# Where the outer sums of a fast matrix product, and the differences of GCN weights, stand in VectorE's queue

## The chip, the cores and the metric

The kernel runs on one core of one Trainium2 chip. The metric is device time of one launch in microseconds (us). TensorE (PE in the profile, PEld for its weight loads) multiplies, VectorE (DVE) and ScalarE (ACT) do elementwise work, GpSimd (POOL) and SyncE (SP) mostly issue DMAs.

## The reference, cut to what matters

Four layers on x of 1250 nodes by 1024 features, each added to its input after a layer norm: a graph attention layer, a feed-forward layer, a graph convolution (GCN) and a mixture of 8 experts. All numbers are float32. The change lies in the second layer and prepares the third:

```python
# feed-forward: two small block-diagonal maps ("rails"), gelu, and one big projection
y = jnp.einsum('btri,hrij->bthrj', xr, rail_maker)
z = jnp.einsum('bthrj,hrkj->bthrk', y, rail_up_proj)
h = jax.nn.gelu(z.reshape(b, t, -1), approximate=False)     # 1250 x 16384
out = h @ w_cproj.T                                         # 1250 x 1024
...
# GCN: one dense 1024 x 1024 map, then a weighted sum over edges
h = jnp.einsum('nd,od->no', x, W) + b
```

## The kernel before, in words

The projection `h @ w_cproj.T` is the longest part: it fills the span from about 420 us to about 2215 us. Its 16384 inner features are cut into `NB` = 16 blocks of 1024. A block is a product of a 1024x1024 weight piece X and a 1024x1250 piece Y of the hidden rows. Both are cut into 2x2 blocks, and each of those into 2x2 again, and the products are taken by Strassen's method (Winograd's form): seven products of sums in place of eight. The outer level's products are numbered p (order `OUTER` = 1, 2, 6, 7, 4, 5, 3), the inner level's i. So a block has 7 x 7 = 49 *steps*, each one call of `product`, with 128x128 by 128x313 matmuls into a PSUM tile `po`. In the last block (number 15, from step `end` = 15 x 49 on) the inner level is done directly, in four steps of two products each for every p.

Three kinds of work go with the steps on VectorE, all of them `tensor_tensor` in float32:

- **Sums ahead of products** (`add_up`, L715): the factors' sums and differences, such as `s1 = 21 + 22`. `projection_plan` gives each a step at which it is to be traced, about 11 us of matmuls ahead of the product that needs it. A 128x512 sum is one of X, a 128x626 one is of Y.
- **Outer sums** (`outer_sums`, L776): the results of the products of blocks 0 to 14 are added up by DMA into the DRAM tensor `acc_d` (`accumulate`: ScalarE copies `po` to SBUF, L731, and a GpSimd DMA adds it, L735). Towards the end each p's seven tiles of `acc_d` are loaded back by `load_sums(p)` (L769, on SyncE's queue) and combined by seven 128x626 additions. The list `bring` says from which step on the additions of each p are traced, and how many a step. In the last block the products are added to these by `combine` (L790 and L795).
- **Differences of GCN weights** (`sum_quarters`, L753 to L756): in blocks 2 to 5 four quarters of the GCN weight are loaded at step 24 of the block (`load_quarters`, L749), and at step 31 four differences of them are taken and written to the DRAM tensor `ws_d` (L758), from where the third layer reads them after the projection.

The tiles share storage: `X`, `low`, `arena`, `BZ` and `first_w` are large SBUF tensors cut into slots (`XS` and `YS`), and the lists `xw` and `yh` hold the free ones. Weights come by SyncE's queue too (`load_weights`, L515). So the order in which slots are given out, and what a slot's next user has to wait for, follow from the order in which the steps are traced.

The order on each engine is not the order of the text. A scheduler that knows estimated times puts the traced instructions into each engine's queue, and it may put one that it thinks ready ahead of others traced before it. An engine then takes its queue strictly in that order: an instruction whose input has not come holds up all that stand behind it. The text can bind the scheduler: inside `with tc.issue_after(ins):` every instruction traced for `ins`'s engine is queued behind `ins`.

Of the kernel before, what the change touches and what calls it, by code (L numbers as in the profile page):

```python
# [15 lines left out]
ALU = mybir.AluOpType  # L16
# [33 lines left out]
OUTER, INNER = (1, 2, 6, 7, 4, 5, 3), (1, 2, 5, 6, 7, 4, 3)  # L50
# [52 lines left out]
def gnn_ffn_kernel(ctx, tc, x, src, dst, gat_w, a_l, a_r, maker, up, cproj,  # L103
# [395 lines left out]
    tt = nc.vector.tensor_tensor  # L499
# [9 lines left out]
    def load_weights(b, o, i):  # L509

        (oo, ok), (io, ik) = corner[o], corner[i]
        r0, c0 = b * D + (2 * ok + ik) * 256, (2 * oo + io) * 256
        k = b, "X", o, i
        buf[k] = xw.pop(0)
        nc.sync.dma_start(XS[buf[k]], cproj[r0:r0 + 256, c0:c0 + 256].rearrange("(q p) o -> p q o", p=P))  # L515
# [29 lines left out]
    with tc.tile_pool(name="aps", bufs=6, space=PSUM) as aps, tc.tile_pool(name="tps0", bufs=2, space=PSUM) as tps:  # L545

        def attend(h, b, between=iter(())):
            po = [aps.tile([R, F + 1], F32, name="po") for _ in range(HT)]
            ws = {}
            for s in range(T):  # L550
                with tc.issue_after(z_copied.ins) if h == b == 0 else nullcontext():
                    ws[s] = first_weights.pop(0) if first_weights else weight(h, b, s)

                for i, v in [(i, s) for i in range(HT)] if s < T - 2 else [(i, v) for i in range(HT) for v in (s - 1, s)] if s == T - 1 else ():
                    nc.tensor.matmul(po[i], ws[v][:, i * R:(i + 1) * R], Z[h // 2][:, v, h % 2, :],
                                                 start=(v == 0), stop=(v == T - 1))
                with tc.issue_after(weighed[-1]):
                    next(between, None)
            rs = small.tile([R, HT], F32, name="rs")

            for group in (range(2), range(2, HT)):
                for i in group:
                    nc.scalar.activation(rs[:, i:i + 1], po[i][:, F:F + 1], AF.Copy, bias=1.0e-30)
                nc.vector.reciprocal(rs[:, group[0]:group[-1] + 1], rs[:, group[0]:group[-1] + 1])
            for i in range(HT):
                xs = X[:, b * HT + i, h * F:(h + 1) * F]
                end = nc.vector.scalar_tensor_tensor(xs, po[i][:, :F], rs[:, i:i + 1], xs, op0=ALU.mult, op1=ALU.add)
            return end
# [19 lines left out]
        with tc.tile_pool(name="al", bufs=2) as lnp:  # L588
# [12 lines left out]
            end = attend(3, 0)  # L601
# [45 lines left out]
    with nullcontext(ctx) as tail:  # L647
# [16 lines left out]
        tt = nc.vector.tensor_tensor  # L664
# [5 lines left out]
        def used(k):  # L670
            left[k] -= 1
            if left[k] == 0:
                (xw if k[1] == "X" else yh).append(buf.pop(k))

        def place_y(top):

            return yh.pop(yh.index(max(yh)) if top else 0)

        def view(k):
            return (XS if k[1] == "X" else YS)[buf[k]]  # L680

        def hidden(b, n, k):

            pz = zps.tile([P, 4, 512], F32, name="pz2")
            for q in range(4):
                hidden_rows(pz[:, q, :NQ], b, n, k, q)
            for i in range(2):
                key = b, "Y", f"{k + 1}{n // 2 + 1}", f"{i + 1}{n % 2 + 1}"
                buf[key] = place_y(b == NB - 1 and n > 1)
                nc.scalar.activation(view(key), pz[:, 2 * i:2 * i + 2, :NQ], AF.Gelu)  # L690
# [19 lines left out]
        def add_up(k, sign, src):  # L710
            a = [view(v) for v in src]
            for v in src:
                used(v)
            buf[k] = xw.pop(0) if k[1] == "X" else place_y(k[0] == NB - 1)
            tt(view(k), *a, op=ALU.add if sign == "+" else ALU.subtract)  # L715

        def product(pairs):
            po = ops.tile([P, 2, 512], F32, name="po2")
# [23 lines left out]
        def quarter(i):  # L742
            return YS[i].rearrange("p q n -> p (q n)")[:, :512]
# [7 lines left out]
        def sum_quarters(k):  # L751
            y11, y21, y12, y22 = (quarter(i) for i in pair)
            tt(y11, y12, y11, op=ALU.subtract)  # L753
            tt(y12, y22, y12, op=ALU.subtract)
            tt(y22, y22, y11, op=ALU.subtract)
            tt(y21, y22, y21, op=ALU.subtract)  # L756
            for j, v in enumerate((y11, y22, y12, y21)):
                nc.sync.dma_start(ws_d[j, k], v)  # L758
            yh.extend(pair)


        def free_acc(v):
            (yh if v < 32 else early).append(v)
# [7 lines left out]
        def outer_sums(p):  # L771

            a = {i: acc.pop((p, i)) for i in INNER}
            for d, x, op, y in ((2, 1, ALU.add, 2), (6, 1, ALU.add, 6), (7, 6, ALU.add, 7), (4, 7, ALU.subtract, 4),
                                (6, 6, ALU.add, 5), (3, 6, ALU.add, 3), (5, 7, ALU.add, 5)):
                tt(YS[a[d]], YS[a[x]], YS[a[y]], op=op)  # L776
                yield
            for i, j in (("11", 2), ("12", 3), ("21", 4), ("22", 5)):
                acc[p, i] = a[j]
            for j in (1, 6, 7):  # L780
                free_acc(a[j])
# [79 lines left out]
        end = (NB - 1) * 49  # L861
        last, j = None, 0
        loads_at = dict(zip((end + v for v in (-13, -6, 1, 7, 12, 15, 20)), OUTER))
        bring = [(end + v, k, outer_sums(w)) for v, k, w in zip((-9, 0, 3, 10, 14, 18, 22), (2, 2, 2, 4, 4, 3, 3), OUTER)]
        added, sent, pair = [], [], []
        norm = {}
        for n, (b, p, i, pairs) in enumerate(steps):
            m = n - 49 * b
            if n >= end - 70:

                xw[:] = [v for v in xw if v < 33]
            for w in (b, b + 1):
                while coming.get(w) and len(xw) > (0 if w == b else 16 if m < 12 else 8 if m < 20 else 4):
                    load_weights(w, *coming[w].pop(0))
            if b == 0:
                for v in first.get(m, ()):
                    hidden(0, *v)
            while j < len(sums) and sums[j][0] <= n:
                add_up(*sums[j][1:])
                j += 1  # L880
            if b == 0 and m in late:
                late_tile(late[m])
                if late[m] == T - 1:
                    xw += range(33, 41)
            if 2 <= b < 6:
                if m == 24:
                    load_quarters(b - 2)
                if m == 31:
                    sum_quarters(b - 2)
            if b + 1 < NB:  # L890
                if m == 20:
                    for k in range(2):
                        load_rails(b + 1, k)
                if m in (28, 30):
                    rails(m // 2 - 14, zps.tile([P, 4, 512], F32, name="pz2")[:, 0, :P])
                if m in later:
                    hidden_visit(b + 1, later[m])
            assert n != end - 13 or all(v < 33 for k, v in buf.items() if k[1] == "X")
            if n in loads_at:
                load_sums(loads_at[n])  # L900
            if n == end:
                blocks.close()
                tl = rest.enter_context(tc.tile_pool(name="tl", bufs=2))
                psp = rest.enter_context(tc.tile_pool(name="tps3", bufs=2, space=PSUM))
                yh += parts
            if b == NB - 1:
                while m >= 14 and [v for v in xw if not 8 <= v < 16] and len(W3) < len(quarters):
                    load_quarter()
                if m == 23:
                    nc.gpsimd.dma_start(bias, gcn_b.partition_broadcast(R))  # L910
                while m >= 16 and len(fetched) < 4 and fetch(len(fetched)):
                    pass
                if m == 22:
                    add_out(0)
                    level(0)
                if m == 24:
                    turn_tile(0)
                if m == 27:
                    add_out(1)
                    level(1)  # L920
                    tt(bias[:, 512:], bias[:, 512:], bias[:, :512], op=ALU.subtract)
            po = product(pairs)
            if last:
                (combine if last[0] == NB - 1 else accumulate)(*last[last[0] == NB - 1:])
            for n0, k, sums_of in bring:
                if n0 <= n:
                    with tc.issue_after(added[-1]) if n > end else nullcontext():
                        for _ in range(k):
                            next(sums_of, None)
            last = b, p, i, po  # L930
# [220 lines left out]
    with back_end:  # L1151
# [160 lines left out]
        with tc.tile_pool(name="ops7", bufs=2, space=PSUM) as ops:  # L1312
# [9 lines left out]
            with tc.If(if_late > 0):  # L1322
                with tc.tile_pool(name="lw", bufs=1) as lwp, tc.tile_pool(name="lps", bufs=1, space=PSUM) as lps:
                    for e in range(NE):
                        a, b, c = w1[e], w2[e], w3[e]
# [66 lines left out]
```

## Time and profile before

| What | Value |
|---|---|
| Time, median of 3 runs | 2744.56 us (2742.64, 2744.56 and 2751.24) |
| The profiled execution's own time | 2747.47 us |
| Its span in the trace | 2745.7 us |
| PE busy | 2709.5 us, 99% of the span |
| DVE busy | 1579.3 us, 58% |
| ACT, POOL busy | 906.2 us and 775.8 us |
| L776 | 49 additions of about 0.80 us, from 2001.0 us to 2201.9 us |
| L753 to L756 | 16 differences of about 0.69 us, from 701.3 us to 1048.0 us |

The span is the time from the first to the last instruction of the trace; the execution's own time is a little longer. Times in a trace are counted from the span's start. In a row of the timeline the first number is the start and the second the duration; what stands in brackets is how long the engine had sat idle before it, and on what it had waited.

### The profile page before, as it was taken

Reading aid. Unit: us, or ns where it says so; the run is one execution under the profiler, and the core shown is the slowest. Engines: PE = TensorE matmul, PEld = TensorE weight load, DVE = VectorE, ACT = ScalarE, POOL = GpSimd, SP = SyncE. Lnnn points to the kernel's source line nnn. Section 1 sums busy time; section 2 is a strip of 40 time slices with the busy share of each in tenths; the row PEclk is TensorE's granted clock in tenths of the full one; section 3 lists DMA queues with packets and bytes.
Section 4 is the critical chain, followed back from the end, with each engine's and each line's share of the span. In section 5 each row is a group of like instructions: output and inputs, shape, how many; then the busy total and the mean of one; then the engine's idle time right before and its main releaser. Section 6 shows DMA issues by size and latency. Waiting matters only on the chain. (4 is left out here: it accounts for less than half of the span.)

```text
span 2745.7 us, 32205 instructions
## 1 busy us (share of the span) xinstructions
PE 2709.5 (99%) x11189; PEld 1893.0 (69%) x11189; DVE 1579.3 (58%) x2708; ACT 906.2 (33%) x1611; POOL 775.8 (28%) x1016
## 2 busy tenths in 40 slices
PE   8999999999999999999999999999999999999998
PEld 6678886676676666766667667666676754675676
DVE  9668988564646556645655556455546765431322
ACT  2333345434434344344343443443432011210000
POOL 2000001243443434434344334343442110112131
PEclk9999999999999999999999999999999999999999
DMA  6336216499999999999999999999998540452784
GB/s 186 92 84 180 71 39 228 164 201 172 210 205 177 227 182 199 199 166 189 190 159 204 179 173 197 166 192 182 143 227 228 169 92 0 87 119 63 270 298 157
DMA packets 269147, 457.74 MB, mean 167 GB/s; under 512 B 53672, under 2 KB 143952, under 8 KB 268593
## 3 DMA queue, kind: packets, MB, share of 16 engines
q0 software_dynamic: 126896, 278.80, 58.7%
q1 hardware_dynamic: 142072, 176.67, 21.4%
q8 instruction: 97, 1.59, 0.2%
q14 instruction: 82, 0.67, 0.1%
HBM read 180.57 MB, written 277.02 MB: 167 GB/s over the span
## 5 line engine op out<-in xcount | busy, mean ns | idle before, releaser
L735 POOL DMA_DIRECT2D acc_d<-low x686 | 589.7, 860 | 914.4 <-ACT low L731 894.1
L731 ACT COPY low<-po 128x626 f32<-128x626 f32 x735 | 501.0, 682 | 952.8 <-PE po L722 891.8
L722 PE MATMUL po<-X,arena 128*128 128x313 f32 x2208 | 619.4, 427 | 0.0
L722 PEld LDWEIGHTS po<-X,arena 128*128 128x128 f32 x2208 | 415.2, 189 | 175.6 <-ACT low L731 16.0
L722 PE MATMUL po<-low,arena 128*128 128x313 f32 x1520 | 429.7, 428 | 0.0
L722 PEld LDWEIGHTS po<-low,arena 128*128 128x128 f32 x1520 | 285.5, 189 | 121.4 <-ACT low L731 11.6
L722 PE MATMUL po<-X,first_w 128*128 128x313 f32 x776 | 222.1, 428 | 1.8 <-DVE X L715 1.8
L722 PE MATMUL po<-X,BZ 128*128 128x313 f32 x720 | 208.5, 433 | 3.6 <-DVE BZ L715 3.6
L722 PEld LDWEIGHTS po<-X,first_w 128*128 128x128 f32 x776 | 145.7, 190 | 64.7 <-ACT low L731 7.6
L722 PE MATMUL po<-low,first_w 128*128 128x313 f32 x624 | 179.5, 429 | 1.0 <-DVE low L715 1.0
L722 PEld LDWEIGHTS po<-X,BZ 128*128 128x128 f32 x720 | 136.9, 192 | 62.6 <-issue 6.1
L722 PEld LDWEIGHTS po<-low,first_w 128*128 128x128 f32 x624 | 117.9, 190 | 50.8 <-ACT low L731 4.4
L227 PE MATMUL pz<-W,xT 128*125 128x256 f32 (+1 forms) x480 | 142.0, 455 | 0.3 <-ACT xT L160 0.3
L715 DVE TENSOR_TENSOR X<-X 128x626 f32<-128x626 f32 x125 | 101.2, 813 | 67.1 <-PE po L722 58.9
L722 PE MATMUL po<-low,BZ 128*128 128x313 f32 x480 | 137.6, 427 | 0.0
L715 DVE TENSOR_TENSOR arena<-arena 128x512 f32<-128x512 f32 x126 | 86.3, 687 | 65.6 <-PE po L722 63.1
L227 PEld LDWEIGHTS pz<-W,xT 128*125 128x125 f32 x480 | 90.0, 190 | 43.8 <-issue 33.8
L715 DVE TENSOR_TENSOR X<-X,low 128x626 f32<-128x626 f32 x105 | 85.3, 816 | 56.2 <-PE po L722 46.0
L722 PEld LDWEIGHTS po<-low,BZ 128*128 128x128 f32 x480 | 90.1, 189 | 38.2 <-ACT low L731 3.7
L715 DVE TENSOR_TENSOR X<-low,X 128x626 f32<-128x626 f32 x101 | 81.7, 813 | 53.3 <-PE po L722 49.0
L707 ACT ACTIVATE X<-pz 128x626 f32<-128x626 f32 (+8 forms) x220 | 101.6, 524 | 17.9 <-PE pz L537 17.9
L715 DVE TENSOR_TENSOR low<-X 128x626 f32<-128x626 f32 x100 | 80.9, 811 | 38.3 <-PE po L722 31.1
(304 smaller groups left out, 3383.6 us busy)
## 6 DMA issues: line engine op xcount, KB each, us to landing
acc_d<-low POOLq DMA_DIRECT2D x735, 313.0 KB, 6.2
arena<-in_cproj SPq DMA_DIRECT2D x148, 256.0 KB
w<-in_w SPq DMA_DIRECT2D x16, 1024.0 KB
BZ<-in_cproj SPq DMA_DIRECT2D x56, 256.0 KB
first_w<-in_cproj SPq DMA_DIRECT2D x52, 256.0 KB
w3t<-in_w SPq DMA_DIRECT2D x8, 1024.0 KB
low<-acc_d SPq DMA_DIRECT2D x19, 313.0 KB
X<-acc_d SPq DMA_DIRECT2D x19, 313.0 KB
```

The costliest lines, as they stand in the source:

```text
L227: made_z = nc.tensor.matmul(pz, xT[:, k, t * R:(t + 1) * R], W[hs[0] // 2][:, k, i:i + len(hs)], start=(k == 0), stop=(k == KD - 1))
L707: nc.scalar.activation(view(key)[:, :, n0 - n * NQ:n1 - n * NQ], pz[:, 2 * i:2 * i + 2, a + n0 - c0:a + n1 - c0], AF.Gelu)
L715: tt(view(k), *a, op=ALU.add if sign == "+" else ALU.subtract)
L722: nc.tensor.matmul(po[:, o, :NQ], view(x)[:, q, o * P:(o + 1) * P], view(y)[:, q, :], start=(i == q == 0), stop=(i + 1 == len(pairs) and q ...
L731: nc.scalar.copy(part, po[:, :, :NQ])
L735: sent[:] = [nc.gpsimd.dma_start(out=acc_d[p - 1, i - 1], in_=part, accum_op=ALU.add).ins]
```

## The change

It does three things. The list `summed` now holds the last instruction that `add_up` traced. The four differences of `sum_quarters` are traced inside `issue_after(summed[-1])`, so they are queued on VectorE behind the sums traced ahead of them. The outer sums of p = 1 are traced from step `end` - 4 on, where it was `end` - 9, and they, too, are queued behind the last sum traced; before step `end` and at it they had been bound to nothing. The outer sums of the other p, which come later, are bound to `combine`'s last addition, as they were. The arithmetic and the number of instructions stay as they were.

```diff
@@ add_up
-            tt(view(k), *a, op=ALU.add if sign == "+" else ALU.subtract)
+            summed[:] = [tt(view(k), *a, op=ALU.add if sign == "+" else ALU.subtract).ins]
@@ the loop's lists
-        bring = [(end + v, k, outer_sums(w)) for v, k, w in zip((-9, 0, 3, 10, 14, 18, 22), (2, 2, 2, 4, 4, 3, 3), OUTER)]
-        added, sent, pair = [], [], []
+        bring = [(end + v, k, outer_sums(w)) for v, k, w in zip((-4, 0, 3, 10, 14, 18, 22), (2, 2, 2, 4, 4, 3, 3), OUTER)]
+        added, sent, pair, summed = [], [], [], []
@@ in the loop over steps
                 if m == 31:
-                    sum_quarters(b - 2)
+                    with tc.issue_after(summed[-1]):
+                        sum_quarters(b - 2)
@@ after the product of a step
                 if n0 <= n:
-                    with tc.issue_after(added[-1]) if n > end else nullcontext():
+                    with tc.issue_after((added or summed)[-1]):
                         for _ in range(k):
                             next(sums_of, None)
```

## The prediction

> **What bounds the kernel now.** I read the page's first part: PE is busy in 99% of the span, and the chain that ended last runs through PE up to 2658 us, with a tail of DMA and GpSimd work behind it. So only what PE waits for is worth anything. The waits of PE by line are therefore next:
>
> ```profile
> PE 2709.5 (99%) x11189; PEld 1893.0 (69%) x11189; DVE 1579.3 (58%) x2708; ACT 906.2 (33%) x1611; POOL 775.8 (28%) x1016
> ```
> ```profile
> PE po L722 <- DVE BZ L715: 3.6, 1, 3.6
> PE pt L159 <- DVE arena L151: 2.5, 1, 2.5
> ...
> PE po L722 <- DVE X L715: 1.8, 1, 1.8
> ...
> PE po L722 <- DVE low L715: 1.0, 1, 1.0
> ```
>
> In the whole projection (L722) PE waited three times, each time for a sum of L715. What held up VectorE? Its timeline before the longest of the three:
>
> ```profile
> 2037.79 0.81 DVE L776 TENSOR_TENSOR low<-arena,low 128x626 f32<-128x626 f32 x1 [15.75 <-DMA low<-acc_d]
> ...
> 2068.76 0.81 DVE L776 TENSOR_TENSOR arena<-arena 128x626 f32<-128x626 f32 x1 [15.06 <-DMA arena<-acc_d]
> 2069.48 0.69 DVE L715 TENSOR_TENSOR first_w<-BZ,arena 128x512 f32<-128x512 f32 x1
> 2071.13 0.81 DVE L776 TENSOR_TENSOR arena<-arena 128x626 f32<-128x626 f32 x1 [0.96 <-DMA arena<-acc_d]
> ...
> 2077.17 0.68 DVE L715 TENSOR_TENSOR BZ<-arena 128x512 f32<-128x512 f32 x1
> ```
>
> VectorE stood still for 15.75 and 15.06 us at outer sums of p = 1 whose tiles had not come back from DRAM, with sums for products queued behind them. The sum ending at 2077.85 is what PE waited for, as PE's timeline shows:
>
> ```profile
> 2072.13 2.27 PE L722 MATMUL po<-X,first_w 128*128 128x313 f32 x8
> 2078.00 4.04 PE L722 MATMUL po<-X,BZ 128*128 128x313 f32 x8 [3.60 <-DVE BZ L715]
> 2081.87 2.27 PE L722 MATMUL po<-X,arena 128*128 128x313 f32 x8
> ```
>
> The two short waits have the other cause. Here are VectorE's and then SyncE's timeline in block 3:
>
> ```profile
> 814.10 0.69 DVE L753 TENSOR_TENSOR X<-X 128x512 f32<-128x512 f32 x1 [9.31 <-DMA X<-in_gcn_w]
> ...
> 823.46 0.69 DVE L754 TENSOR_TENSOR X<-X 128x512 f32<-128x512 f32 x1 [5.42 <-DMA X<-in_gcn_w]
> ...
> 826.12 0.81 DVE L715 TENSOR_TENSOR low<-low,X 128x626 f32<-128x626 f32 x1
> ```
> ```profile
> 799.08 5.78 SPq L749 DMA_DIRECT2D X<-in_gcn_w  x3
> 814.82 0.33 SPq L758 DMA_DIRECT2D ws_d<-X  x1
> 815.24 0.38 SPq L749 DMA_DIRECT2D X<-in_gcn_w  x1
> ```
>
> The fourth quarter's load stands on SyncE's queue behind the write of the first difference, which waits for L753. So VectorE waits twice in a row, and PE then waits for the sum at 826.12.
>
> **The change, part by part.** No instruction is added or removed; the built order of both programs tells what moves.
>
> *Differences of weights.* On VectorE L753 moves behind five sums, which had run at 814.71 to 817.36. They now fit into the 9.31 us before L753 (five at 0.6 to 0.7 us: 3.5 us). On SyncE the four loads become neighbours; the first write (L758) moves behind the two weight loads that followed (816.75 and 817.18), so it goes out some 3 us later. Nobody waits for it: `ws_d` is read after the projection. The two weight loads lose a blocker.
>
> When does the fourth load land? Not shown in this place, so I bound it. From below: the time from issue to the end of VectorE's wait for it, 8.2 us here (815.24 to 823.46) and 7.4 us in block 4. From above: 16.5 us, block 4's longest (first load issued 910.48, L753 started 926.96). The third issue ends at 804.86, so the landing lies between 812.3 and 821.4, plus whatever its slot makes it wait; I take the middle, 817. The need: PE could have begun the waiting product at 825.87 (a group of two L532 matmuls before it takes 0.21 us, as at 821.22). In the new order L754 is followed by a sum, L755 and the sum needed, which ends 2.75 us after L754's start; PE starts 0.14 us after that (826.93 to 827.07). So L754 may start as late as 823.0, and even the upper bound leaves 1.6 us. The wait goes. Block 4 has the same order of instructions; its deadline is 937.28 - 2.89 = 934.4 against 916.3 + 16.5 = 932.8. Start to start PE lost 827.07 - 825.87 = 1.20 us and 939.26 - 937.28 = 1.98 us, and each first group after it ran 0.08 us slow (2.19 for 2.11 us). Gain: **3.34 us**. In blocks 2 and 5 PE did not wait: 0.
>
> *Outer sums of p = 1.* All seven move behind the sum that stood at 2079.10 in VectorE's queue. Each sum that was held up at 2037.79 and 2068.76 now goes ahead, the one ending at 2077.85 among them. It needs only weights and sums; between 2053.6 and 2068.76 VectorE was idle, and the ten sums from 2069.48 up to it take 0.6 to 0.7 us each, 6.6 us, so it is done by about 2060, or when its slot comes free. PE's wait goes. Start to start PE lost 2078.00 - 2074.24 = 3.76 us. The next eight matmuls took 3.87 us where 2.11 us is the rule, since the granted clock was low (0.79 on average in 2074 to 2082): 1.76 us more. Gain: **5.52 us**.
>
> What is late next? Behind and among the outer sums stand seven more 128x512 sums of the last blocks (0.61 us apart). If the last tile lands at 2071.13 as before, the seven outer sums (0.73 us each), one outer sum of p = 2 and these seven end at 2071.1 + 5.8 + 4.3 = 2081.2; before, the last of them ended at 2085.7. The last block's first product was at 2092.8, and with 8.9 us gained it is at 2083.9. So 2.7 us remain if the loads come no earlier. They should: SyncE reached them (2058.94) only after a 9.02 us issue of a weight load at 2049.80, which follows PE's progress. The other 42 outer sums stay bound to `combine`. At the step `end` itself p = 2's outer sums were free and are now bound to the last sum; their tiles landed just in time (waits of 0.62 and 0.74 us), and I price that at 0, with 1 us each way.
>
> *The clock.* After the 3.60 us gap the clock was halved; it was halved too after the 2.53 us gap at 2195 (0.76 in 2195 to 2202), and not after gaps of 1.03 and 1.81 us. That third gap I leave: VectorE is busy 4.95 of 5 us before it, with the last tiles' additions and a layer norm, which the change does not touch. [...]
>
> *Sum.* 3.34 + 5.52 = 8.86 us of the profiled execution's 2747.47 us. Everything after 2215 us hangs on PE's progress and follows. That execution is 2.9 us above the median of the runs. The runs lie 8.6 us apart, and waits for DMAs that end just in time are the likely reason. I take the gain off the median: 2744.56 - 8.86 = **2735.7 us**; off the profiled execution it is 2738.6 us.
>
> **Rivals.**
>
> *The outer sums' wait only moves.* The tiles land later than 2071.1 by more than the margin of 2.7 us, since the DMA engines are busy throughout there (share 1.08 in 2074 to 2082), and last-block products wait in place of the earlier one. For: loads before had waits of 15 us. Against: the sums at stake come 4.5 us earlier than before with unchanged landings. At 8 us late PE loses the 5.3 us beyond the margin, and the time is 2735.7 + 5.3 = 2741.0 us.
>
> *The fourth quarter becomes the wait, in four blocks: slower.* All sums behind L754 now wait in one place. If the load lands d us after 823.0 and its like in blocks 2, 4 and 5, PE loses d each time: 4d - 8.86. That decides against the kernel from d = 2.2 us, and by over 0.3% from 4.3 us, a landing 22.4 us after the third issue. At d = 6 us: 2759.7 us. For it: block 4's 16.5 us come within 1.6 us of the deadline, and a slot that frees late adds to it. Against: no load of this kind in the trace took 17 us.
>
> *The change does nothing that lasts.* The profiled waits are of that execution alone and typical ones have fewer: 2744.6 us. Against it: the queue order that makes them is fixed at build time.
>
> **How the numbers follow.** About 0.3% (8.2 us) is what a measurement of this kernel can tell from no change: bounds 2736.3 and 2752.8 us. The forecast gets 0.72; its own range is 2732 (the low clock at 2198 goes as well, 1.8 us, and loads that free up VectorE another 2) to 2738.6 us, and I put 0.54 beyond the bound and 0.18 within it, since executions with longer waits than the profiled one (2751.24 us) gain more. The moved wait gets 0.14, all within. The fourth quarter gets 0.10, slower; nothing that lasts 0.04, half of it within and half slower. So faster 0.54, same 0.34, slower 0.12. The range is 2731 to 2743 us: it takes in the forecast's and the moved wait's times with the unknown 1 us on either end, and leaves out the slow case.
>
> **What would show it.** In the profile after: no wait of PE at L722 for L715; in the blocks 2 to 5 one wait at L753, and one of at most 3 us at L754; four loads L749 as neighbours on SyncE; all outer sums of p = 1 in one stretch at about 2060 to 2076 us with PE busy throughout; the granted clock 1.00 from 423 to 2190 us. I am wrong if PE waits near 2085 to 2100 us, or at L754's place in several blocks, or if PE's gaps go and the time stays.

## The result, and the profile after

| | Before | After |
|---|---|---|
| Time, median | 2744.63 us (22 runs, 2739.6 to 2755.9) | 2754.25 us (22 runs, 2738.88 to 2778.6) |
| Ratio after to before | | 1.0044, 95% interval 1.0028 to 1.006 |
| Profiled execution | 2747.47 us, span 2745.7 us | 2747.03 us, span 2745.3 us |
| PE busy | 2709.5 us | 2707.5 us |
| POOL busy | 775.8 us | 790.0 us |

The change made the kernel slower by 0.44%, where a gain was forecast. Two things in the table point at the cause before any row is read: the times after are spread over 40 us where those before were spread over 16, and GpSimd, whose multiplications the prediction never looked at, is busy for 14.2 us more with the same instructions.

The waits of PE by line, in the profile after (total, times, longest):

```profile
PE po L722 <- ACT low L731: 9.1, 1, 9.1
...
PE pt L159 <- DVE arena L151: 1.1, 1, 1.1
```

The three waits for sums of L715 are gone, as predicted. In their place stands one wait of 9.05 us, for a copy of ScalarE. The chain behind it is followed back engine by engine. PE's timeline in block 5, then ScalarE's:

```profile
1052.59 2.27 PE L722 MATMUL po<-low,arena 128*128 128x313 f32 x8
1063.92 4.28 PE L722 MATMUL po<-low,BZ 128*128 128x313 f32 x8 [9.05 <-ACT low L731]
1068.03 2.27 PE L722 MATMUL po<-X,arena 128*128 128x313 f32 x8
```
```profile
1050.73 0.68 ACT L731 COPY low<-po 128x626 f32<-128x626 f32 x1 [1.43 <-PE po L722]
1063.18 0.68 ACT L731 COPY low<-po 128x626 f32<-128x626 f32 x1 [11.78 <-DMA acc_d<-low]
```

ScalarE had to empty `po` for PE, but it had no free slot to copy into: the slots are given back by the DMAs that add them to `acc_d`. Those are issued by GpSimd. Its timeline:

```profile
1040.70 0.86 POOL L735 DMA_DIRECT2D acc_d<-low  x1 [1.25 <-ACT low L731]
1042.07 14.75 POOL L524 TENSOR_TENSOR BZ<-BZ 128x128 f32<-128x128 f32 x1 [0.51 <-PE pz L532]
1056.79 0.83 POOL L526 TENSOR_TENSOR BZ<-BZ 128x128 f32<-128x128 f32 x1
1057.57 1.76 POOL L735 DMA_DIRECT2D acc_d<-low  x2
```

L524 is a small multiplication of GpSimd in `load_rails`: it spreads a piece of the next block's rail weights over a mask (L526 does the same for the second map). It took 14.75 us. In the profile of before none of the 64 executions of L524 and L526 took over 1.05 us. Behind it in the queue stood the accumulating DMAs, which PE needs every 2.1 us. What did VectorE do meanwhile?

```profile
1036.98 0.69 DVE L754 TENSOR_TENSOR X<-low,X 128x512 f32<-128x512 f32 x1 [3.72 <-DMA low<-in_gcn_w]
1037.59 0.80 DVE L715 TENSOR_TENSOR low<-X 128x626 f32<-128x626 f32 x1
...
1042.39 0.69 DVE L715 TENSOR_TENSOR arena<-arena,first_w 128x512 f32<-128x512 f32 x1
...
1055.87 0.69 DVE L715 TENSOR_TENSOR first_w<-arena,BZ 128x512 f32<-128x512 f32 x1
1056.59 0.77 DVE L715 TENSOR_TENSOR BZ<-arena,first_w 128x512 f32<-128x512 f32 x1
```

It ran sums and differences with two inputs in SBUF, one at the heels of the other, for some 19 us. A 128x512 sum starts 0.60 us after the last one when nothing holds it; the one at 1056.59 reads what the one before wrote and starts after 0.72 us. GpSimd's multiplication ends there, at 1056.82. In the profile of before, the same multiplication and VectorE's neighbours of it are, on GpSimd and on VectorE:

```profile
1045.28 0.40 POOL L524 TENSOR_TENSOR BZ<-BZ 128x128 f32<-128x128 f32 x1 [0.51 <-PE pz L532]
```
```profile
1039.93 0.68 DVE L715 TENSOR_TENSOR BZ<-arena 128x512 f32<-128x512 f32 x1
1045.77 0.83 DVE L754 TENSOR_TENSOR X<-low,X 128x512 f32<-128x512 f32 x1 [5.16 <-DMA low<-in_gcn_w]
```

Before, L524 ran at 1045.28, inside VectorE's 5.16 us of waiting for the fourth quarter. It did so in block 3 (821.7 us) and block 4 (933.1 us) as well. After, in block 5, L754 comes about 9 us earlier, VectorE is through with its waiting when L524 becomes ready, and L524 meets the run of sums. That alone does not hold it: `load_rails` runs twice for each block, and in the profile of before the first L524 of block 2 (711.5 us) and the second one of all four blocks ran beside sums and took 0.62 to 1.05 us. What else it takes, the bench below shows.

The price is read from the starts in PE's timeline: 1063.92 - 1052.59 = 11.33 us where 2.11 us is the rule (9.22 us lost), and 1068.03 - 1063.92 = 4.11 us for the next group at about half the clock (0.53 granted in that stretch; 2.00 us lost). One held multiplication costs **11.2 us**. The windows, with the columns start and end, length, busy time (instructions) of PE, PEld, DVE, ACT and POOL, granted clock, DMA share and GB/s, show the two losses side by side:

```profile
1054.00:1064.00 10.00, 0.95 (x5) 0.38 (x3) 5.06 (x8) 0.68 (x1) 8.70 (x9) 0.68 0.54 98
1064.00:1074.00 10.00, 10.00 (x34) 6.31 (x35) 1.39 (x2) 4.32 (x8) 3.40 (x4) 0.81 1.12 204
```

**Theory A** for the experiments: GpSimd's multiplication is held off by VectorE's unbroken run, and the wait that the change shortens and moves had been its cover. **Theory B**: the outer sums cost the time. **Theory C**, on the bench: beside VectorE, GpSimd loses one instruction's length at most.

### The profile page after: what moved, and what is told of

Same layout as the page of the kernel before. It is cut to its first block, busy times and chain, and to the rows that moved or that the text cites. A ratio compares the mean times of both kernels' runs of the same rounds, so it can differ in the third digit from the quotient of the medians.

```text
span 2745.3 us, 32206 instructions
## 1 busy us (share of the span) xinstructions
PE 2707.5 (99%) x11189; PEld 1891.5 (69%) x11189; DVE 1581.5 (58%) x2708; ACT 906.3 (33%) x1611; POOL 790.0 (29%) x1016
## 5 line engine op out<-in xcount | busy, mean ns | idle before, releaser
L722 PE MATMUL po<-X,arena 128*128 128x313 f32 x2200 | 616.8, 427 | 0.0
L722 PEld LDWEIGHTS po<-X,arena 128*128 128x128 f32 x2200 | 413.8, 189 | 174.8 <-ACT low L731 16.0
L722 PE MATMUL po<-low,arena 128*128 128x313 f32 x1528 | 431.6, 428 | 0.0
L722 PEld LDWEIGHTS po<-low,arena 128*128 128x128 f32 x1528 | 287.0, 189 | 122.0 <-ACT low L731 11.6
L722 PE MATMUL po<-X,first_w 128*128 128x313 f32 x784 | 223.3, 428 | 0.0
L722 PE MATMUL po<-X,BZ 128*128 128x313 f32 x720 | 206.5, 430 | 0.0
L722 PEld LDWEIGHTS po<-X,first_w 128*128 128x128 f32 x784 | 147.1, 189 | 63.1 <-ACT low L731 7.6
L722 PEld LDWEIGHTS po<-X,BZ 128*128 128x128 f32 x720 | 136.0, 191 | 58.2 <-ACT low L731 5.8
L722 PE MATMUL po<-low,first_w 128*128 128x313 f32 x616 | 175.6, 427 | 0.0
L722 PEld LDWEIGHTS po<-low,first_w 128*128 128x128 f32 x616 | 116.0, 189 | 48.9 <-ACT low L731 4.4
L722 PE MATMUL po<-low,BZ 128*128 128x313 f32 x480 | 139.6, 432 | 9.1 <-ACT low L731 9.1
L715 DVE TENSOR_TENSOR X<-X 128x626 f32<-128x626 f32 x125 | 101.3, 814 | 74.2 <-PE po L722 66.0
L715 DVE TENSOR_TENSOR arena<-arena 128x512 f32<-128x512 f32 x126 | 86.8, 690 | 69.2 <-PE po L722 66.7
L722 PEld LDWEIGHTS po<-low,BZ 128*128 128x128 f32 x480 | 91.1, 192 | 48.3 <-ACT low L731 13.2
L715 DVE TENSOR_TENSOR X<-X,low 128x626 f32<-128x626 f32 x106 | 85.7, 811 | 56.7 <-PE po L722 46.0
L715 DVE TENSOR_TENSOR X<-low,X 128x626 f32<-128x626 f32 x100 | 81.2, 817 | 53.4 <-PE po L722 49.0
L715 DVE TENSOR_TENSOR low<-X 128x626 f32<-128x626 f32 x99 | 80.2, 813 | 38.3 <-PE po L722 31.1
```

Source lines behind the costliest of these rows:

```text
L715: summed[:] = [tt(view(k), *a, op=ALU.add if sign == "+" else ALU.subtract).ins]
L722: nc.tensor.matmul(po[:, o, :NQ], view(x)[:, q, o * P:(o + 1) * P], view(y)[:, q, :], start=(i == q == 0), stop=(i + 1 == len(pairs) and q ...
```

## The experiments

### One half of the change each

The kernel with only the outer sums moved and tied (`outer_only`), against the changed kernel:

```diff
-                    with tc.issue_after(summed[-1]):
-                        sum_quarters(b - 2)
+                    sum_quarters(b - 2)
```

> Only the outer sums of p = 1 are moved and tied; the differences of the GCN weights stay where they were in the kernel before. Theory A (a multiplication of the rails on GpSimd, L524, cannot start while VectorE runs sums without a break, and the accumulating DMAs behind it on GpSimd then come late; it was 14.75 us in the changed kernel's block 5, where the differences' wait no longer breaks VectorE's run): the differences' waits and their short PE gaps of 1 to 2 us are back, no L524 above about 1.1 us, no PE gap near 2075 us, so the 5.5 us of that gap are gained: about 2739 us. Theory B (the moved outer sums themselves cost the time, by late tiles or by DMA traffic near the end): as slow as the changed kernel, about 2754 us.

Measured: 2739.87 us (12 runs), ratio 0.9992 to before, interval 0.9982 to 1.0003. Its profile has one wait of PE in the projection, one of the short ones for the differences:

```profile
PE po L722 <- DVE X L715: 0.9, 1, 0.9
```

The kernel with only the differences tied (`quarters_only`):

```diff
-...zip((-4, 0, 3, 10, 14, 18, 22), (2, 2, 2, 4, 4, 3, 3), OUTER)]
+...zip((-9, 0, 3, 10, 14, 18, 22), (2, 2, 2, 4, 4, 3, 3), OUTER)]
...
-                    with tc.issue_after((added or summed)[-1]):
+                    with tc.issue_after(added[-1]) if n > end else nullcontext():
```

> Only the differences of the GCN weights are tied behind the sums; the outer sums stay as before. Theory A: this part carries the whole loss; L524 takes many times its 0.4 to 1 us in some of the blocks 2 to 5, in some executions and not in others, PE waits there for ScalarE's copies, and PE's gap near 2075 us stays: about 2754 + 5 = 2759 us, with runs some 20 us apart. Theory B: 2744.6 - 3.3 = 2741 us, runs close together.

Measured: 2754.35 us (11 runs, 2741.81 to 2778.33), ratio 1.0036, interval 1.0018 to 1.0054: all of the changed kernel's loss and all of its spread. Its profiled execution was its slowest, 2778.33 us, with three held multiplications (15.78, 16.19 and 15.48 us in the blocks 2, 4 and 5) and these waits of PE:

```profile
PE po L722 <- ACT low L731: 30.1, 3, 10.4
PE po L722 <- DVE BZ L715: 3.0, 1, 3.0
```

The second row is the wait behind the outer sums, which this kernel leaves as they were. So theory B falls: the loss comes from the differences' tie alone, and the outer sums' half is harmless at least.

### The changed kernel once more

No edit; a second profile.

> The changed kernel as it is, for a second profile. Theory A: for each multiplication of the rails that takes over 10 us, TensorE has a gap of 9 to 10.5 us in the same block, and the span is the 2735 us that the kernel has without any, plus about 12 to 14 us for each (the gap and the half clock after it). Theory B (the outer sums cost the time): the span does not go with the number of held multiplications.

Measured: 2758.82 us, span 2757.1 us, two held multiplications. GpSimd's timeline in blocks 4 and 5:

```profile
930.57 14.62 POOL L524 TENSOR_TENSOR BZ<-BZ 128x128 f32<-128x128 f32 x1
...
1052.38 15.49 POOL L524 TENSOR_TENSOR BZ<-BZ 128x128 f32<-128x128 f32 x1 [0.51 <-PE pz L532]
```

PE's gaps behind them are 8.85 and 9.72 us. The span is 11.8 us above that of the first profile, which has one. At 11.2 us each, the runs from 2738.88 to 2778.6 us would be runs with none to three or four, out of the four blocks that have differences, and the median one with one or two; only the profiled ones show their number.

### The masks multiplied on VectorE

The changed kernel, and then the kernel before, with L524 and L526 moved:

```diff
-        nc.gpsimd.tensor_tensor(mb.rearrange("p (a b) -> p a b", a=8), ...
+        nc.vector.tensor_tensor(mb.rearrange("p (a b) -> p a b", a=8), ...
...
-        nc.gpsimd.tensor_tensor(ub.rearrange("p (a b) -> p a b", a=2), ...
+        nc.vector.tensor_tensor(ub.rearrange("p (a b) -> p a b", a=2), ...
```

> The changed kernel, with the two multiplications of load_rails (L524 and L526) on VectorE in place of GpSimd, 64 instructions in all. Theory A: GpSimd now only issues DMAs in the projection and is not held up; no PE wait for a copy of L731; what the prediction added up is there: 2735 to 2739 us, runs within some 5 us. Theory B, or any theory in which DMA traffic or the order of the loads delays the accumulating DMAs: still about 2754 us with a wide spread. Against A would also be a GpSimd DMA issue (L735) that takes several us.

Measured: 2735.5 us (7 runs, 2732.58 to 2739.41), ratio 0.9971, interval 0.9958 to 0.9984. No product of the projection (L722) stands among PE's waits. On VectorE each L524 takes 0.28 us; its row in the answer by line (min/median/max in ns):

```profile
L524 DVE TENSOR_TENSOR BZ<-BZ x32: 278/283/286, 326.8 to 1930.5; 128x128 f32<-128x128 f32 x32
```

> The kernel before, with the two multiplications that load_rails gives to GpSimd (the masks of the rails) given to VectorE instead; nothing else. In the trace of before these multiplications of the blocks 2 to 5 ran while VectorE waited 4.6 to 5.5 us for its fourth quarter, and none took over 1.05 us. Theory A (GpSimd's multiplication is held by VectorE's unbroken run, and the wait that the change removes had been its cover): before has nothing to win here, its three waits of TensorE (1.03, 1.81 and 3.60 us) stay, and the time stays within 0.3% of before: 2738 to 2752 us. Theory C (VectorE is simply the better place for these multiplications, and the 2735.5 us of the changed kernel with them on VectorE owe nothing to the change): about as fast as that one, 2732 to 2739 us.

Measured: 2740.43 us (12 runs), ratio 0.9991, interval 0.998 to 1.0002. Theory A had said that all three waits of PE stay; in the profiled execution only the one near 2074 us was there, with 1.44 us. The two short ones had gone (0.2 us was left) though VectorE still waited before L754 (3.93 us in block 3, 5.66 us in block 4). Theory A's reading of before, that the multiplications of the blocks 2 to 5 ran inside VectorE's waits, holds for the first pair in blocks 3 to 5 alone. As these waits come and go from run to run, the two kernels were then put side by side:

> The changed kernel with the rails' masks multiplied on VectorE, once more, now on the same chip and in the same rounds as its counterpart without the change. If the change is worth what its removed waits of TensorE amount to once GpSimd is out of the way, this stays at 2733 to 2738 us and some 5 us under its counterpart; if the place of the multiplications had made all of the gain, the two are within 2 us of each other.

> The counterpart: the kernel before with the same multiplications on VectorE. Its wait of TensorE near 2074 us and VectorE's waits for the fourth quarter are still there: 2739 to 2743 us if the change is what gains, 2734 to 2738 us if the place of the multiplications is.

Measured in the same rounds: 2734.4 us with the change (6 runs, 2732.3 to 2736.95, ratio to before 0.9958, interval 0.9941 to 0.9975), 2741.38 us without it (12 runs, 2734.37 to 2748.64, ratio 0.9987, interval 0.9974 to 1.0). With GpSimd out of the way the change is worth 2741.38 - 2734.40 = 7.0 us by the medians; the runs of the two overlap, and the two intervals just touch. The place of the multiplications alone is worth 2.8 and 3.1 us by the medians of its two rounds, with intervals that reach to no gain. The waits in the kernel without the change, in this profile:

```profile
PE po L722 <- DVE BZ L715: 4.4, 1, 4.4
PE po L722 <- DVE X L715: 2.0, 1, 2.0
```

With the change none of them is there. The changed kernel with the masks on VectorE has the lowest median of all versions, and both its intervals lie below the time of before.

### The multiplications queued behind an accumulating DMA

The changed kernel, with the masks still on GpSimd but queued behind the last accumulating DMA traced before them, around product 20 of the 49 in a block:

```diff
-                    for k in range(2):
-                        load_rails(b + 1, k)
+                    with tc.issue_after(sent[0]) if sent else nullcontext():
+                        for k in range(2):
+                            load_rails(b + 1, k)
```

> The changed kernel with the masks of the rails still multiplied on GpSimd, but bound behind the last accumulating DMA that GpSimd issues in the block up to product 20, so that no such DMA of this block stands behind them in GpSimd's queue. Theory A: some multiplications are still held for 10 to 16 us beside VectorE's run, but nothing that TensorE waits for stands behind them; the gaps of 9 to 10 us go, and the time is 2734 to 2742 us. If instead the hold of GpSimd also keeps back the accumulating DMAs that are already issued (their descriptors), or the next block's first accumulation, the gaps of 9 us stay and the time is that of the changed kernel, 2748 to 2760 us.

Measured: 2740.16 us (12 runs, 2735.56 to 2744.3), ratio 0.9983, interval 0.9974 to 0.9993. The time is as theory A had it, but not the way there: no multiplication was held for 10 us. The longest took 4.29 us, in several blocks, and ended where VectorE ran out of work. GpSimd's timeline and VectorE's in block 1:

```profile
585.59 4.29 POOL L524 TENSOR_TENSOR BZ<-BZ 128x128 f32<-128x128 f32 x1
589.86 0.39 POOL L526 TENSOR_TENSOR BZ<-BZ 128x128 f32<-128x128 f32 x1
...
591.48 3.52 POOL L735 DMA_DIRECT2D acc_d<-low  x4
```
```profile
588.94 0.68 DVE L715 TENSOR_TENSOR arena<-BZ 128x512 f32<-128x512 f32 x1
590.35 0.93 DVE L715 TENSOR_TENSOR low<-low,X 128x626 f32<-128x626 f32 x1 [0.72 <-PE po L722]
```

The edit does not do what was expected of it: later accumulating DMAs of the block still stand behind the multiplications, as the four from 591.48 us on show; PE did not wait for them. It also made the multiplications run earlier in the block (1031.94 us in block 5, before VectorE waits for the quarters). So the kernel lost its long holds by where the multiplications now fall, beside short runs, and it does not tell whether a long hold would have been harmless there. The profile also shows the rival of the late fourth quarter once: in block 2, L754 started at 718.87 us after a wait of 9.13 us, and PE waited 3.98 us. There the built order had put the rails' four loads among the quarters on SyncE's queue.

### A bench for the hold itself

The first bench (`lock_bench`) computes none of the layers.

> None of the layers is computed: the kernel only measures a small GpSimd multiplication (128x128, one operand broadcast, float32, in SBUF), started at 21 different phases within a run of 20 VectorE instructions of 128x626 or 128x512 float32. Theory A: alone it takes about 0.4 us; beside independent two-input additions, back to back, some of them take the rest of the run, 10 us or more; beside additions that each wait for the one before (a small break between them), or one-input multiplications, at most 1 to 2 us. Rival C (GpSimd waits for one VectorE instruction at most, and the 14.75 us were something else): never above about 1.2 us in any of them. The 8 GpSimd DMAs issued beside such a run show whether issuing is held up too: 0.86 us each if not.

Measured: alone the multiplication took 0.39 to 0.40 us. Beside 20 adds it took by turns 0.4 to 1.05 us and 13.89 to 14.25 us (128x626), or 11.50 to 11.89 us (128x512); its arrival was shifted by about 0.04 us from run to run, over some 0.8 us, and that did not change the turns. GpSimd's issue of a DMA beside such a run took 0.54 us: that was not held. Its segments with a chain and with one input were mixed by the scheduler, so they do not tell the two kinds apart (the multiplication was held there for up to 22.14 us), and the bench was built again:

> A bench that computes none of the layers: VectorE adds of 128x626 in runs, each of whose first reads what GpSimd's last multiplication (128x128) wrote, and one GpSimd multiplication that becomes ready at the start of each run. Order of the runs: 3 with no adds; 10 of 20 adds; 10 of 21; 6 of 22; 10 of 20 and 6 of 21 with two multiplications; 8 of 20 adds that each read the one before; 8 of 20 where each fourth reads the one before; 8 of 20 multiplications by a constant (one input); 8 of 20 with one operand in PSUM; 4 of 20 adds with a multiplication of 512 columns. Theory A: beside independent adds with two inputs in SBUF the multiplication takes either 0.4 to 1.1 us or the rest of the run (13 to 15 us); beside a chain it takes 0.4 to 1.1 us each time, since VectorE pauses before each add; with a dependent add each fourth, no hold is longer than four adds (about 3 us). If the long holds go by the number of VectorE's instructions, those of the 21 and 22 runs come in another order than those of the 20 runs; if by GpSimd's own instructions, all alternate alike, and with two multiplications in each run the same one of them is always the held one. If only the length of the run counts, every first multiplication is held. One input or an operand in PSUM: no hold by the theory that two readers of SBUF collide (0.4 to 1.1 us each); a hold as long as the run by the theory that any unbroken run does it.

Measured: alone 0.40 us. Beside 20, 21 and 22 independent adds 0.57 us and 14.27, 14.99 or 15.71 us, strictly by turns. With two multiplications a run, either both pass (0.57 and 0.96 us) or the first is held for 14.27 us and the second comes after the run. Beside a chain 0.51 and 0.61 us, never held. With a dependent add every fourth: 2.73 us in six of eight, else 0.57 us. One input: 7.74 us and 0.64 us by turns, so it does not take two inputs. One operand in PSUM: 0.40 us each time. In the last four runs only ScalarE's copy ahead of the multiplication was 512 columns wide, the multiplication was not: 13.95 and 0.97 us by turns. GpSimd's and VectorE's timeline of a held one and the one after it, which passes, one beside a chain and one with an operand in PSUM:

```profile
28.80 0.16 DVE L123 TENSOR_TENSOR start<-back,a 128x16 f32<-128x16 f32 x1
28.89 14.49 DVE L129 TENSOR_TENSOR b<-a,a 128x626 f32<-128x626 f32 x20
...
29.37 14.27 POOL L139 TENSOR_TENSOR back<-gi,go 128x128 f32<-128x128 f32 x1 [14.13 <-ACT go L125]
43.67 0.18 DVE L123 TENSOR_TENSOR start<-back,a 128x16 f32<-128x16 f32 x1 [0.29 <-POOL back L139]
...
44.26 0.57 POOL L139 TENSOR_TENSOR back<-gi,go 128x128 f32<-128x128 f32 x1 [0.62 <-ACT go L125]
...
677.00 3.42 DVE L133 TENSOR_TENSOR chain<-chain,a 128x626 f32<-128x626 f32 x4
...
677.46 0.61 POOL L139 TENSOR_TENSOR back<-gi,go 128x128 f32<-128x128 f32 x1 [16.39 <-ACT go L125]
...
995.07 3.07 DVE L137 TENSOR_TENSOR b<-pp,a 128x512 f32<-128x512 f32 x5
...
995.56 0.40 POOL L139 TENSOR_TENSOR back<-gi,go 128x128 f32<-128x128 f32 x1 [11.64 <-ACT go L125]
```

Theory C falls: the hold lasted as long as VectorE went on without a pause, 14.27 us over 20 instructions. It ended at the first add that waited for the one before (after 2.73 us with one every fourth), as at 1056.59 us in the kernel.

The turns are made by the bench itself. After a multiplication that passed, VectorE goes into the next run without a pause (28.80 us), and the next multiplication is held; a held one makes VectorE wait for it (0.29 us before 43.67 us), and the next one passes. So, by the traces, it goes with how long VectorE has run without a pause when the multiplication starts. Beside independent adds in SBUF, every multiplication that started within 1.2 us of a pause passed, and every one that started 12.9 us or more after it was held. With a dependent add every fourth, of seven that started 3.47 us after it six were held.

The kernels agree, and there GpSimd's own idle time, which on the bench goes with the turns (14.13 us before the held one shown, 0.62 us before the other), was about 0.5 us before held and passed ones alike. I count from VectorE's last pause, or from GpSimd's multiplication before if that came later, since it delays VectorE too (in the profile after, the 128x626 sum at 717.64 us took 1.00 us beside the L526 of 717.14 us, and the next one 0.80 us). In the projections of the seven profiles with the masks on GpSimd, fifteen multiplications were held for 3.0 us or more, they started 3.64 to 6.25 us after it, and each ended 0.26 us after the last VectorE instruction ahead of the next pause. Of those that met sums and passed, all but one started up to 3.55 us after it (the one, in `after_rails_late` at 2023.39 us, 4.35 us). In the profile after, the first L524 of blocks 2, 3 and 4 started after 3.29, 3.55 and 3.20 us and passed, that of block 5 after 5.09 us and was held. No run varied this time alone, so the bound near 3.5 us is read off, not tested.

### The kernel before once more

> The kernel before as it is, for a second profile: several of its runs lie at 2750 to 2756 us, where most lie at 2740 to 2746 us. If those are runs in which its second pair of multiplications in a block, which does run beside VectorE's sums, is held, a profile of such a run has one or more multiplications of over 5 us and a gap of TensorE behind it; in a profile at 2740 to 2746 us there is none. One look may fall on either side.

Measured: 2739.5 us, no multiplication over 1.08 us. PE's waits in the projection were 1.06, 1.05 and 1.43 us, where the first profile had 1.03, 1.81 and 3.60. Whether the runs of before at 2750 to 2756 us hold a multiplication, this profile does not tell; it stays open.

## Why the prediction was wrong

**What bounds the kernel, and the three waits: right.** All three of PE's waits for sums went, and the clock was full in the projection (1.00 granted from 423 to 1050 us and from 1070 to 2190 us) except in the new gap and behind it (0.65 from 1054.90 to 1063.92 us, 0.53 from there to 1068.03 us).

**The differences of weights: the order was right, the step that followed from it wrong.** The four loads are neighbours (one issue group of 10.00 us from 799.17), and the fourth quarter landed in time. In block 3:

```profile
818.24 0.69 DVE L754 TENSOR_TENSOR X<-X 128x512 f32<-128x512 f32 x1 [3.44 <-DMA X<-in_gcn_w]
```

That is 818.24 against the estimate of 817 and the deadline of 823.0; the waits before L754 were 3.4 to 3.9 us, a little over the 3 us that I had named. The step that failed is "The wait goes. [...] Gain: 3.34 us", with "In blocks 2 and 5 PE did not wait: 0." It asked who waits for VectorE, and not who works while VectorE stands still. VectorE's wait was the cover of GpSimd's L524. With the wait over about 9 us earlier in block 5, L524 started 5.09 us into an unbroken run and was held for 14.75 us, and this block, priced at 0, lost 11.2 us. The part "What is late next?" was asked for the outer sums alone, and of the queues that the differences were moved past only SyncE's was looked at. The term is not a saving of 3.34 us but, by `quarters_only` against its runs of before, 2754.35 - 2742.95 = 11.4 us lost.

**The outer sums: right in kind, too large.** The tied sums ran first and the outer sums came in one stretch at the end, with later sums between them:

```profile
2070.05 0.68 DVE L715 TENSOR_TENSOR BZ<-first_w,arena 128x512 f32<-128x512 f32 x1
2074.34 1.53 DVE L776 TENSOR_TENSOR arena<-arena 128x626 f32<-128x626 f32 x2 [3.60 <-DMA arena<-acc_d]
...
2080.47 0.81 DVE L776 TENSOR_TENSOR arena<-low,arena 128x626 f32<-128x626 f32 x1
```

They were done by 2081.3 us, not 2076, since the last tiles landed at about 2074.3, and the sums by 2070.7 us, not 2060: at 2062.80 one waited 2.62 us for its weights. PE did not wait for any of it, so the margin held. But the 5.52 us were sized by one execution. The wait that was 3.60 us there was 1.43, 1.44, 3.02 and 4.45 us in other profiles with the old order, and the half clock of 1.76 us did not come with every wait: the granted clock was 0.93 in 2100 to 2125 us of `quarters_only`, around the wait of 3.02 us, but 1.00 from 939 to 943 us of before, behind the wait of 1.81 us. Measured for this half: 2742.95 - 2739.87 = 3.1 us, with an interval that touches zero.

**The gap left alone.** The wait at L159 near 2197 us, which the prediction took as untouched, was 2.53 us before and 1.10 us after, and 1.23 us in the second profile of before: it varies by itself.

**The rivals.** The slower case had chance 0.12, and its mechanism was another one, the fourth load. No rival looked at GpSimd, though it issues the DMAs that free ScalarE's slots, and the profile of before showed its multiplications inside VectorE's waits in three of the four blocks. The rival that nothing lasts was dismissed because the queue order is fixed when the kernel is built; the order is, but the waits that it makes are not, as the second profile of before showed. The sum of 8.86 us itself was not far off for a kernel without that conflict: 7.0 us measured there. That such a kernel takes 2734.4 to 2735.5 us, beside the 2735.7 us predicted, is in part luck, since the outer sums brought 3.1 of their 5.52 us and the move of the masks may have brought some 3 us that the sum did not have.

## What to carry to other kernels

A wait that is removed was time in which another engine could work: look up which instructions of the other engines lie inside it, and what stands behind these in their queues. Keep elementwise work of GpSimd out of a queue that issues DMAs on the way of a bottleneck engine when VectorE runs long trains of independent operations on SBUF; in this kernel 0.28 us on VectorE was cheaper than 0.40 us on GpSimd with a risk of 11 us. Ask not only whether such a train is there, but how long it has run when GpSimd's instruction comes. And a gap seen in one profile is sized from several before it is sold as a gain.

## What the runs showed of the hardware that was not expected

- A GpSimd multiplication of 0.40 us beside an unbroken run of VectorE operations on SBUF took as long as the rest of the run (11.50 to 15.71 us beside 20 to 22 adds on the bench, 14.62 to 16.19 us in the profiles `after`, `after_again` and `quarters_only`), and ended at the first VectorE instruction that paused. On the bench, runs of two-input adds in SBUF held it (14.27 us), and so did runs of one-input multiplications (7.74 us); adds with one operand in PSUM did not (0.40 us). The hold was not one instruction's: it spanned 20.
- It did not happen each time, and it went with how long VectorE had run without a pause. On the bench all multiplications beside independent adds passed within 1.2 us of a pause, and all were held from 12.9 us on; in the kernels they passed up to 3.55 us after it, with one exception, and were held from 3.64 us on. In the profile of before, the second pair of each block came 1.36 to 3.10 us after it and passed (L524 took 0.62 to 1.05 us).
- The granted clock halved for 3.4 us after gaps of PE of 2.53 and 3.60 us (before: 0.50 from 2198 to 2201 us, 0.56 from 2078.0 to 2081.9 us) and stayed at 1.00 after gaps of 1.03 and 1.81 us (before). Behind the gap of 9.05 us (after) it was half for 10.2 us, about 6 us of them in the gap itself (0.68 from 1054 to 1064 us, 0.81 from 1064 to 1074 us).
